# A bilinear stage moved onto column quarters of the matmul array

## The chip, the cores and the metric

The kernel runs on one core of one Trainium2 chip. The time is device microseconds of one launch; the kernel before took 5544.77 us (median of three runs, 5533.71 to 5545.04). The execution that the profile shows spans 5535.1 us. A core has five engines with a queue each: TensorE for matrix products (PE in the profile; its weight loads are shown apart as PEld), VectorE (DVE), ScalarE (ACT), GpSimd (POOL) and SyncE (SP), which here only issues transfers (DMA). They run side by side and wait for each other by semaphores. Data for the engines lie in SBUF, 128 partitions wide; TensorE writes its results to PSUM, which has 128 partitions too.

## The reference

The program is a chain of four layers on an image batch of shape 4 x 96 x 64 x 64. Layer 0 is a state-space block, layers 2 and 3 are a Fourier attention with a feed-forward block. The change concerns layer 1 alone, a bilinear form in every pixel:

```python
s = jax.lax.reduce_window(x, 0.0, jax.lax.add, window_dimensions=(1, 1, K, K), ...)
p = s / float(K * K)
...
p = p.reshape(n, c, ho * wo).transpose(0, 2, 1)
wm = weight * mask
t = jnp.einsum('nlc,ocd->nlod', p, wm)
y = jnp.einsum('nlod,nld->nlo', t, p)
y = y + bias[None, None, :]
```

For each of 4 x 4096 pixels and each of 96 outputs o, y is the sum over all channel pairs (c, d) of wm[o, c, d] p[c] p[d]. The input x is group-normalised first, and y is added to x.

## The kernel before, in words

Since p[c] p[d] is symmetric, the weights of (c, d) and (d, c) are added, and 4656 distinct pairs are left. The kernel holds p as 96 rows (channels) by 4096 columns (pixels) of an image in DRAM, stored twice one below the other, so that rows can be read turned round by any number of channels. Twelve turned copies of 128 rows (`_TURNS`, tiles `turn0` to `turn11`) are loaded for a block of columns. A product of two such copies, element by element, holds p[c] p[d] for 128 channel pairs at once; `_PAIRS` lists the 37 products (copy 0 with itself, then each of copies 6 to 11 with each of copies 0 to 5) that meet every pair. A matmul with 128 rows of weights (`wk`, 37 sets of 128 x 96) sums a product into the 96 outputs; 37 of them accumulate in PSUM.

In `_bilinear` the stage first builds `wk` from weights and masks (L550 to L559). Then it goes over the four images and, in each, over blocks of `CW` = 1024 columns. A block loads its twelve turned copies (L567 and L568, two transfers each, two sets of buffers, so that the next block loads beside the present one). For each k of 37, VectorE multiplies two copies into z (L577; ScalarE squares copy 0 at L575), and two matmuls of 512 columns each (L580) take it up. There are three z buffers. At the block's end VectorE adds the sum and a bias to the image's features (L581). When an image is done, TensorE transposes it in pieces (L587), ScalarE copies them out of PSUM (L588), and a transfer writes them to `tok`.

The order of each engine's queue in this stage is not written out by hand: a scheduler of the framework orders ready instructions by its own model of costs, and puts in the semaphores between tiles. Only the first stage (`_mamba`) writes its order by hand. That stage also holds the one place where two matmuls use different column ranges of the array: `proj` (L214) computes 64 outputs to partitions 0 to 63 and another 64 to partitions 64 to 127 of one PSUM tile.

Of the kernel before, what the change touches and what calls it, by code (L numbers as in the profile page):

```python
# [9 lines left out]
F32 = mybir.dt.float32  # L10
# [3 lines left out]
AF = mybir.ActivationFunctionType  # L14
ALU = mybir.AluOpType
# [4 lines left out]
B, C, L = 4, 96, 4096  # L20
# [9 lines left out]
HID = 384  # L30
NHC = HID // 128
EPS = 1e-5
CW = 1024

# [1 line left out]
_TURNS = [(s, (32 * (i % 3) + 16 * (i // 3)) % C) for i, s in enumerate((0, 76, 60, 44, 32, 88))]  # L38
_TURNS += [(s, 32 * (i % 3) + (2, 6)[i // 3]) for i, s in enumerate((25, 1, 73, 49, 24, 48))]
_PAIRS = [(0, 0)] + [(i, j) for j in range(6, 12) for i in range(6)]  # L40
# [491 lines left out]
def _bilinear(ctx, tc, io, w, f_all, p2, tok):  # L532

    nc = tc.nc
    wp = ctx.enter_context(tc.tile_pool(name="bw", bufs=1))
    stage = ctx.enter_context(tc.tile_pool(name="bst", bufs=1))
    turned = ctx.enter_context(tc.tile_pool(name="bturn", bufs=2))
    work = ctx.enter_context(tc.tile_pool(name="bwork", bufs=3))  # L540
    ps = ctx.enter_context(tc.tile_pool(name="bps", bufs=2, space=PSUM))
    ps_t = ctx.enter_context(tc.tile_pool(name="bpst", bufs=2, space=PSUM))
    bias = w["vec"][:, _V_L1B : _V_L1B + 1]

    NK = 4
    NT = len(_PAIRS)
    wk = wp.tile([128, NT, C], F32, name="wk", tag="wk")
    for k0 in range(0, NT, NK):
        e = min(k0 + NK, NT)
        part = []  # L550
        for n in "12":
            wt = stage.tile([128, NK, C], F32, name=f"wt{n}_{k0}", tag=f"wt{n}")
            mt = stage.tile([128, NK, C], F32, name=f"mt{n}_{k0}", tag=f"mt{n}")
            nc.sync.dma_start(wt[:, : e - k0, :], io["bw" + n][:, k0:e, :])
            nc.sync.dma_start(mt[:, : e - k0, :], io["bm" + n][:, k0:e, :])
            out = wk[:, k0:e, :] if n == "1" else wt[:, : e - k0, :]
            nc.vector.tensor_tensor(out, wt[:, : e - k0, :], mt[:, : e - k0, :], ALU.mult)
            part.append(wt)
        nc.vector.tensor_tensor(wk[:, k0:e, :], wk[:, k0:e, :], part[1][:, : e - k0, :], ALU.add)  # L559

    for b in range(B):
        for q in range(L // CW):
            cols = slice(q * CW, (q + 1) * CW)
            rows = []
            for i, (hi, lo) in enumerate(_TURNS):
                t = turned.tile([128, CW], F32, name=f"turn{i}_{b}_{q}", tag=f"turn{i}")
                nc.sync.dma_start(t[0:C, :], p2[b][hi : hi + C, cols])  # L567
                nc.sync.dma_start(t[C:128, :], p2[b][lo : lo + 128 - C, cols])  # L568
                rows.append(t)
            p_y = ps.tile([C, CW], F32, name=f"py2_{b}_{q}", tag="py2")  # L570
            for k, (i, j) in enumerate(_PAIRS):
                z = work.tile([128, CW], F32, name=f"z_{b}_{q}_{k}", tag="z")
                m = C if i == j else 128
                if i == j:
                    nc.scalar.activation(z[:m], rows[i][:m], AF.Square)  # L575
                else:
                    nc.vector.tensor_tensor(z, rows[i], rows[j], ALU.mult)  # L577
                for n in range(CW // 512):
                    ns = slice(n * 512, (n + 1) * 512)
                    nc.tensor.matmul(p_y[:, ns], wk[:m, k, :], z[:m, ns], start=(k == 0), stop=(k == NT - 1))  # L580
            nc.vector.scalar_tensor_tensor(f_all[b][:, cols], p_y, bias, f_all[b][:, cols], ALU.add, ALU.add)  # L581
        xv = f_all[b].rearrange("c (i j) -> c j i", j=NJ)
        tt = stage.tile([128, NJ, C], F32, name=f"tt{b}", tag="tt", bufs=1)
        for j0 in range(0, NJ, 4):
            p_t = ps_t.tile([128, 4, C], F32, name=f"pt_{b}_{j0}", tag="pst")
            for j in range(4):
                nc.tensor.transpose(p_t[:, j, :], xv[:, j0 + j, :], w["ident"][:C, :C])  # L587
            nc.scalar.copy(tt[:, j0 : j0 + 4, :], p_t)  # L588
        nc.sync.dma_start(tok[b], tt)


def _tokens(ctx, tc, io, w, tok, out):
# [287 lines left out]
@with_exitstack  # L880
def kernel(ctx: ExitStack, tc: tile.TileContext, io, out):
    nc = tc.nc
    cp = ctx.enter_context(tc.tile_pool(name="common", bufs=1))
    dp = ctx.enter_context(tc.tile_pool(name="scratch", bufs=1, space=DRAM))
    w = _shared(nc, cp, io)
    p2 = [dp.tile([2 * C, L], F32, name=f"p2_{b}", tag=f"p2_{b}") for b in range(B)]
    tok = [dp.tile([128, NJ, C], F32, name=f"tok_{b}", tag=f"tok_{b}") for b in range(B)]
    fd = [dp.tile([C, L], F32, name=f"fd_{b}", tag=f"fd_{b}") for b in range(B)]
    with tc.tile_pool(name="stats", bufs=1) as fp:
        fstats = fp.tile([C, B, NCH, 6], F32, name="fstats", tag="fstats")  # L890
        xstats = fp.tile([C, B, NCH, 6], F32, name="xstats", tag="xstats")
        with ExitStack() as c:
            _mamba(c, tc, io, w, fd, fstats, xstats)
        with tc.tile_pool(name="features", bufs=1) as fp2:
            f_all = [fp2.tile([C, L], F32, name=f"f_{b}", tag=f"f_{b}") for b in range(B)]
            with ExitStack() as c:
                _norms_and_pool(c, tc, io, w, f_all, fd, fstats, xstats, p2)
            with ExitStack() as c:
                _bilinear(c, tc, io, w, f_all, p2, tok)
    with ExitStack() as c:  # L900
        _tokens(c, tc, io, w, tok, out)
# [135 lines left out]
```

## Time and profile before

| what | value |
|---|---|
| median time | 5544.77 us |
| span of the profiled execution | 5535.1 us |
| TensorE busy over the span | 4498.7 us (81%) |
| VectorE busy over the span | 4279.5 us (77%) |
| GpSimd busy over the span | 3057.4 us (55%) |
| ScalarE busy over the span | 2553.0 us (46%) |
| first and last start of L580 | 3152.7 and 4221.9 us |
| mean of one multiply L577 (128 x 1024) | 1224 ns |
| mean of one eviction L581 (96 x 1024) | 1280 ns |
| mean of one transpose copy L588 (128 x 384) | 478 ns |

How to read it: an engine's busy share is an average over stages with different limits, so it does not tell what bounds one stage. The profile also gives groups of instructions by line (busy time, mean time of one, and the idle time of the engine just before them with what ended it), the chain of work that ended last, and the busy time of each engine in any stretch of the span. An fp32 matmul stands in the trace as two records of a weight load and a stream each, so that 1184 matmuls of L580 are 2368 records. The end of a matmul in the trace is modelled; the steps from start to start are the safer measure.

### The profile page before, as it was taken

The page shows a single profiled execution, that of the slowest core. Times are in us where ns is not written, and L with a number is a line of the kernel's source. Part 1 is how long each engine was busy: PE and PEld are TensorE (multiplying, and loading weights), DVE is VectorE, ACT ScalarE, POOL GpSimd, SP SyncE. Part 2 cuts the span into 40 slices and gives each one's busy share as a digit, 9 for nine tenths or more (in the row PEclk, how much of TensorE's full clock was granted, in tenths as well). Part 3 has the DMA queues.
Part 4 walks back from the last instruction along what each step waited for, and adds up shares of the span by engine and source line. Part 5 has one row for each costly group of instructions (what it writes and reads, how often), then busy time and mean ns, then how long its engine had stood idle before and what let it go on. Part 6 is the DMA issues. An engine that isn't in the chain of part 4 may idle for free. (4 is left out here: it accounts for less than half of the span.)

```text
span 5535.1 us, 44436 instructions
## 1 busy us (share of the span) xinstructions
PE 4498.7 (81%) x12740; PEld 2034.8 (37%) x12740; DVE 4279.5 (77%) x5316; ACT 2553.0 (46%) x5337; POOL 3057.4 (55%) x2193
## 2 busy tenths in 40 slices
PE   7888888989888988888883099999996777767674
PEld 2333333333333333333321033333332665556462
DVE  5999999999999999999999667767676455556363
ACT  5666767676767666666663000000000434343444
POOL 5999999999999999999994000000000222231313
PEclk9999999999999999999996599999997877768686
DMA  4534444443535353535353463443322000000001
GB/s 97 112 86 102 100 98 104 91 107 87 112 79 123 74 127 68 127 70 124 70 122 107 146 160 99 109 106 95 107 76 80 17 16 16 16 16 16 16 12 46
DMA packets 112892, 461.33 MB, mean 83 GB/s; under 512 B 22660, under 2 KB 30278, under 8 KB 77704
## 3 DMA queue, kind: packets, MB, share of 16 engines
q1 hardware_dynamic: 112648, 458.51, 34.8%
q8 instruction: 100, 1.64, 0.1%
q14 instruction: 144, 1.18, 0.1%
HBM read 422.78 MB, written 35.65 MB: 83 GB/s over the span
## 5 line engine op out<-in xcount | busy, mean ns | idle before, releaser
L373 POOL TENSOR_TENSOR dbx<-du,bq 128x1024 f32<-128x1024 f32 x768 | 1803.2, 2353 | 3.3 <-DMA bq<-rows 3.2
L394 PE MATMUL py<-hc,ident 128*128 128x512 f32 x3072 | 1600.6, 626 | 137.9 <-DVE hc L383 110.6
L367 ACT ACTIVATE da<-delta,aneg 128x512 f32<-128x512 f32 x1536 | 1058.9, 691 | 91.5 <-DVE hs L380 71.5
L380 DVE TENSOR_TENSOR_SCAN da<-da,hst,dbx 128x512 f32<-128x512 f32 x864 | 1099.2, 1272 | 1.2 <-POOL dbx L373 1.2
L580 PE MATMUL py<-z,wk 128*96 128x512 f32 (+1 forms) x2368 | 1022.6, 594 | 82.8 <-DMA mt<-in_bm 43.9
L394 PEld LDWEIGHTS py<-hc,ident 128*128 128x128 f32 x3072 | 554.6, 195 | 1098.3 <-issue 530.9
L383 POOL TENSOR_TENSOR hc<-hs,cq 128x512 f32<-128x512 f32 x672 | 852.9, 1269 | 187.3 <-DVE hs L380 98.6
L577 DVE TENSOR_TENSOR z<-turn,turn 128x1024 f32<-128x1024 f32 x576 | 702.8, 1224 | 302.3 <-PE py L580 276.6
L380 DVE TENSOR_TENSOR_SCAN hs<-da,hst,dbx 128x512 f32<-128x512 f32 x672 | 856.0, 1274 | 9.0 <-ACT da L367 9.0
L707 POOL MEMSET lnT<- 1x512 f32 x64 | 33.2, 520 | 1309.5 <-PE py L580 1237.1
L383 DVE TENSOR_TENSOR hc<-da,cq 128x512 f32<-128x512 f32 x864 | 597.6, 692 | 80.8 <-DMA cq<-rows 4.2
L580 PEld LDWEIGHTS py<-z,wk 128*96 128x96 f32 (+1 forms) x2368 | 386.3, 164 | 709.4 <-issue 624.0
L575 ACT ACTIVATE z<-turn 96x1024 f32<-96x1024 f32 x16 | 16.9, 1056 | 998.9 <-PE py L580 956.5
L387 ACT COPY hst<-da 128x1 f32<-128x1 f32 x864 | 136.2, 158 | 728.1 <-DVE hc L383 718.6
L230 PE MATMUL pc<-xs,taps 128*128 128x512 f32 x768 | 380.7, 592 | 0.0
L840 POOL TENSOR_TENSOR t<-t,o 128x384 f32<-128x384 f32 x64 | 60.3, 942 | 474.9 <-DVE o L838 474.9
L689 POOL TENSOR_SCALAR x_a<-t,m_a,r_a 128x96 f32<-128x96 f32 x256 | 105.6, 427 | 319.8 <-PE plt L705 277.7
L741 PE MATMUL px<-mats,a 128*128 128x128 f32 x768 | 182.4, 403 | 72.6 <-DVE a L730 40.9
L204 PE MATMUL pr<-r,picks 128*96 128x512 f32 x128 | 111.1, 970 | 151.6 <-DVE r L200 151.6
L230 PEld LDWEIGHTS pc<-xs,taps 128*128 128x128 f32 x768 | 145.5, 190 | 185.0 <-issue 174.7
L712 PE MATMUL ph<-w,lnT 97*128 97x192 f32 x512 | 158.5, 478 | 65.6 <-ACT lnT L708 40.3
L214 PE MATMUL pxz<-hn,in_w 96*64 96x512 f32 x768 | 211.6, 622 | 0.0
(231 smaller groups left out, 5179.3 us busy)
## 6 DMA issues: line engine op xcount, KB each, us to landing
bq<-rows SPq DMA_DIRECT2D x256, 512.0 KB, 6.6
cq<-rows SPq DMA_DIRECT2D x256, 512.0 KB, 10.1
turn<-p SPq DMA_DIRECT2D x192, 384.0 KB, 5.6
turn<-p SPq DMA_DIRECT2D x192, 128.0 KB, 5.8
p<-pt SPq DMA_DIRECT2D x8, 1536.0 KB, 10.7
k_fwd<-in_k_fwd SPq DMA_DIRECT2D x32, 256.0 KB, 2.7
k_inv<-in_k_inv SPq DMA_DIRECT2D x32, 256.0 KB, 2.8
x<-in_x SPq DMA_DIRECT2D x16, 384.0 KB, 5.0
```

The costliest lines, as they stand in the source:

```text
L214: nc.tensor.matmul(q[h, :], in_w[:, l, 64 * kk : 64 * kk + 64], hn[b], start=True, stop=True)
L230: nc.tensor.matmul(p_c[k], taps[:, (l * 3 + k) * 4 + j, :], xs[k][:, j : j + TC], start=(j == 0), stop=(j == 3))
L367: nc.scalar.activation(da[u], st[n]["delta"][k], AF.Exp, scale=aneg[:, at : at + 1])
L373: nc.gpsimd.tensor_tensor(t, st[n]["du"][k].unsqueeze(1).to_broadcast([128, 2, TC]), b, ALU.mult)
L380: nc.vector.tensor_tensor_scan(hs[u], da[u], dbx[u], hst[:, at : at + 1], ALU.mult, ALU.add)
L383: (nc.gpsimd if on_pool(u) else nc.vector).tensor_tensor(hc[u], hs[u], c, ALU.mult)
L387: nc.scalar.copy(hst[:, at : at + 1], hs[u][:, TC - 1 : TC])
L394: nc.tensor.matmul(py[n, k], ident, hc.pop(u), start=(s == 0), stop=(s == 15))
L577: nc.vector.tensor_tensor(z, rows[i], rows[j], ALU.mult)
L580: nc.tensor.matmul(p_y[:, ns], wk[:m, k, :], z[:m, ns], start=(k == 0), stop=(k == NT - 1))
L712: nc.tensor.matmul(p_h[:, jj, :], lnT[:, j + jj, :], d["w1"], start=True, stop=True)
L741: nc.tensor.matmul(p_x[:, k, :], a2[:, 128 * m : 128 * m + 128, k0 + k], bd0 if k0 + k == 0 else bd, start=True, stop=True,)
```

## The change

A matmul with 96 outputs uses 96 of the array's 128 columns. The change splits each product into three of 32 outputs, one per column quarter (PSUM partitions 0 to 31, 32 to 63 and 64 to 95), and gives the free fourth quarter (partitions 96 to 127) to the last nine of the 37 products: their three groups of 32 outputs make 27 products of 32, one for each of the first 27 passes. So 28 passes of up to four products are meant to do what 37 did.

The last nine z tiles (the late tiles) are made by GpSimd, one block ahead, and are kept for the whole block. Their sums gather in three PSUM tiles (`acc[0]` to `acc[2]`, all in partitions 96 to 127); ScalarE copies them to `ev`, GpSimd adds `ev` to the features, and VectorE adds the rest as before. Blocks are 512 columns instead of 1024, loads are issued a block ahead, there are four z buffers, and an image's transposes stand after pass 8 of the next image's first block. The three lines of a pass that carry it are L615 (three products of z), L618 (one of a late tile) and L626 (the copy of a finished group).

```diff
-CW = 1024
+CW = 512
...
-    for b in range(B):
-        for q in range(L // CW):
...
-            p_y = ps.tile([C, CW], F32, name=f"py2_{b}_{q}", tag="py2")
-            for k, (i, j) in enumerate(_PAIRS):
-                z = work.tile([128, CW], F32, name=f"z_{b}_{q}_{k}", tag="z")
-                m = C if i == j else 128
-                if i == j:
-                    nc.scalar.activation(z[:m], rows[i][:m], AF.Square)
-                else:
-                    nc.vector.tensor_tensor(z, rows[i], rows[j], ALU.mult)
-                for n in range(CW // 512):
-                    ns = slice(n * 512, (n + 1) * 512)
-                    nc.tensor.matmul(p_y[:, ns], wk[:m, k, :], z[:m, ns], start=(k == 0), stop=(k == NT - 1))
-            nc.vector.scalar_tensor_tensor(f_all[b][:, cols], p_y, bias, f_all[b][:, cols], ALU.add, ALU.add)
+    NP = 28
+    NX = NT - NP
...
+    def make_late(n):
+        k = NP + len(late[n])
+        i, j = _PAIRS[k]
+        z = work.tile([128, CW], F32, name=f"z_{n}_{k}", tag=f"z{k}")
+        nc.gpsimd.tensor_tensor(z, rows[n][i], rows[n][j], ALU.mult)
+        late[n].append(z)
...
+    for n, (b, q) in enumerate(blocks):
+        cols = slice(q * CW, (q + 1) * CW)
+        if n + 1 < len(blocks):
+            load(n + 1)
+        acc = [ps.tile([128, CW], F32, name=f"py{g}_{n}", tag=f"py{g}") for g in range(3)]
+        ev = work.tile([C, CW], F32, name=f"ev_{n}", tag="ev")
+        for p in range(NP):
...
+            z = work.tile([128, CW], F32, name=f"z_{n}_{p}", tag="z", bufs=4)
...
+            for g in range(3):
+                gs = slice(32 * g, 32 * g + 32)
+                nc.tensor.matmul(acc[0][gs, :], wk[:m, p, gs], z[:m], start=(p == 0), stop=(p == NP - 1))
+            if p < 3 * NX:
+                g, k = divmod(p, NX)
+                nc.tensor.matmul(
+                    acc[g][96:128, :],
+                    wk[:, NP + k, 32 * g : 32 * g + 32],
+                    late[n][k],
+                    start=(k == 0),
+                    stop=(k == NX - 1),
+                )
+                if k == NX - 1:
+                    nc.scalar.copy(ev[32 * g : 32 * g + 32, :], acc[g][96:128, :])
+            if n + 1 < len(blocks) and p % 3 == 2:
+                make_late(n + 1)
+            if p == 8 and q == 0 and b > 0:
+                transposes(b - 1)
+        nc.gpsimd.tensor_tensor(f_all[b][:, cols], f_all[b][:, cols], ev, ALU.add)
+        nc.vector.scalar_tensor_tensor(f_all[b][:, cols], acc[0][:C, :], bias, f_all[b][:, cols], ALU.add, ALU.add)
+    transposes(B - 1)
```

## The prediction

> **What bounds the kernel now.** I read the page's costliest groups and its chain first, because the change is confined to one stage (lines 540 to 589) and the question is what that stage waits for.
>
> ```profile
> PE py L580 18%; PE ph L712 2%; PE px L741 2%; PE pa L721 1%; PE pf L833 1%; DVE a L730 1%; ACT y L826 1%; DVE hq L829 1%; PE pv L772 1%; PE plt L705 1%; POOL x_f L689 1%; PE pv L776 1%; DVE r L827 1%; PE pg L791 1%; PE poo L800 1%
> ...
> L580 PE MATMUL py<-z,wk 128*96 128x512 f32 (+1 forms) x2368 | 1022.6, 594 | 82.8 <-DMA mt<-in_bm 43.9
> ...
> L577 DVE TENSOR_TENSOR z<-turn,turn 128x1024 f32<-128x1024 f32 x576 | 702.8, 1224 | 302.3 <-PE py L580 276.6
> ```
>
> One line, the matrix product of L580, is 18% of the chain that ended last. VectorE, which makes its inputs, is busy 702.8 us and idle 302.3 us in the stage, mostly waiting for TensorE to give a z buffer back. Next I cut the stage into stretches; the columns are busy us and count of PE, PEld, DVE, ACT and POOL, then the granted clock.
>
> ```profile
> core 0: us, PE busy (x) PEld busy (x) DVE busy (x) ACT busy (x) POOL busy (x), PEclk, DMA share, GB/s
> ...
> 3400.00:3600.00 200.00, 200.00 (x492) 78.17 (x491) 139.73 (x115) 6.88 (x11) 0.00 (x0) 1.00 0.38 103
> 3600.00:3800.00 200.00, 200.00 (x491) 78.19 (x490) 139.60 (x115) 6.88 (x11) 0.00 (x0) 1.00 0.40 105
> ```
>
> TensorE is busy 200 of 200 us at full clock, GpSimd 0, ScalarE 7, DMA at 0.4. The stage is a bare stream of matmuls from 3195 to 4222 us. An fp32 matmul shows as two records (two loads of weights, two streams). The median step from one record to the next is 0.429 us, so a product of 512 columns costs **0.858 us**, whatever number of outputs it has: 16 blocks x 37 pairs x 2 halves = 1184 products x 0.858 = 1016 us of the stage's 1027.
>
> So the count of 0.858 us slots decides the stage. Does the trace show products side by side in the array? Only for two, in the first stage: L214 writes two sets of 64 outputs, to partitions 0 and 64.
>
> ```profile
> 1521.97 1.08 PE L214 MATMUL pxz<-hn,in_w 96*64 96x512 f32 x4
> 1522.97 2.84 PE L394 MATMUL py<-hc,ident 128*128 128x512 f32 x6
> 1525.75 1.08 PE L214 MATMUL pxz<-hn,in_w 96*64 96x512 f32 x4
> 1526.76 1.13 PE L394 MATMUL py<-hc,ident 128*128 128x512 f32 x2
> 1527.72 0.59 PE L230 MATMUL pc<-xs,taps 128*128 128x512 f32 x1
> ```
>
> Four records (two products) are through in 1.00 us, 1.08 with the tail; a lone product that follows (1526.76) takes 0.96 us to the next. Over all 192 pairs the second product starts a median 7 ns after the first. Two products in different column groups cost one slot.
>
> **What the Trainium skill says.** TensorEngine Tiling (Array Packing), Key Properties: tiles work independently, and changing the mode, not the tile, drains the array. The pairs above agree. TensorE: Matmul & The Clock Gate, Part 3, Measured speedup: three column tiles of 32 outputs ran 2.38 times as fast; no row here has three or four. The same page, What overlaps and what doesn't: matmuls start in program order, strict FIFO. PSUM — Partial Sum Buffer, Engine vs sequencer instructions, says the same of start and completion. The pairs neither prove nor break this for long runs: they only show a neighbour starting 7 ns later.
>
> **The change, part by part.**
>
> (1) Slots intended: 28 passes per 512 columns, each with four products of 32 outputs (three from z_p, one from a late tile), instead of 37 products of 96. At 0.858: 32 blocks x 28 = 896 slots, 769 us.
>
> (2) Slots as queued. This is the step on which the forecast stands. The source puts a late product into each of passes 0 to 26, but the instructions go through a scheduler, and TensorE's queue in the built program is different. In a typical block it holds nine passes of four, then **18 late products in a row** (the last two sets of nine), then 19 passes of three. Around the four image ends the grouping shifts (35 in a row, or blocks with 16), with the same sums. The reason shows in the queue: pass 9's first product waits for a semaphore of ScalarE besides VectorE's. The copy of the finished quarter (acc[0], partitions 96 to 127) at L626 stands before it, as the tile is the same one; the scheduler filled that wait with everything that was ready.
>
> All 18 write partitions 96 to 127. They need the same column group one after another, and with starts in order nothing passes them. Per block: 9 + 18 + 19 = 46 slots; the first triple can start beside the last late product (as the pairs of L214 do): 45. 45 x 32 = 1440 against 1184: 256 more x 0.858 = **+220 us**.
>
> (3) Passes of three or four cost one slot? Lower bound 0.858, the stream. Upper bound: two at a time, as proven here, 1.72. The skill's 2.38 for three speaks for all at once; loads of 32 columns are shorter than the 163 ns of 96. I take 0.858.
>
> (4) VectorE: 27 multiplies of 512 per block. L383 has this shape on VectorE at 692 ns beside a busy GpSimd: 27 x 0.692 = 18.7 us, plus the eviction (1.28 us for 1024 columns, so some 0.75): 19.4 us against 45 x 0.858 = 38.6. Hidden behind TensorE, with four z buffers ahead. In the queue it does two multiplies of the next block before it waits in the eviction, so TensorE has passes 0 to 2 to eat meanwhile: nothing queued behind that wait is late.
>
> (5) GpSimd: nine multiplies and one add per block; L383 on GpSimd, same shape, is 1269 ns: 10 x 1.27 = 12.7 us in 38.6, hidden. Late tiles wait for rows loaded a block ahead. Those issues stand behind the previous block's last multiplies and come at about 0.7 us each in the steady part (pairs every 1.4 to 1.7 us), so the last five pairs land some 10 us into the block, and the late tiles are ready about 13 us in; the earliest late product hoisted from the next block comes 25 slots (21 us) in. No wait.
>
> (6) ScalarE: three copies of 32x512 (L588 copies 384 columns in 478 ns, so about 0.6 each) and a square: 2.5 us, hidden by the 18 late products.
>
> (7) DMA: same bytes, half as long rows; 3.1 MB in 38.6 us is 81 GB/s against 103 now. Hidden.
>
> (8) Ends. The first block waits for half the rows; at the 223 GB/s of the start that would be 14 us, but weights for all pairs are needed by the first pass, so I take 7. In the first nine passes late tiles come at 1.27 us, not 0.86: 9 x 0.41 = +4. Block seams 32 times instead of 16, with a semaphore hop: an estimate of +8 in all (0.15 to 0.3 each). Sum +5.
>
> Sum: 5545 + 220 (2) + 0 (3 to 7) + 5 (8) = 5770; the seams may partly hide behind z buffers that stand ready, so I say **5765 us**, 4% slower.
>
> **The rivals.**
>
> Deep overtaking, faster: the array holds a long reorder window and starts the triples beside the 18 late products. Then all 28 passes count: 32 x 28 = 896 slots, 288 fewer x 0.858 = -247, so **5300**. For it: the intent, independent tiles, and the fact that two records per product still let the neighbour start 7 ns later. Against: both pages state program order, and that neighbour is all that is shown. 14%.
>
> Partial overtaking: the skill (TensorE: Matmul & The Clock Gate, Architectural detail) gives the queue 64 entries with partial reordering. With load and matmul that is 16 products; while 18 late ones drain, about five triples get in: 41 slots, 1312, 128 more: +110, **5655**. If entries count only matmuls, ten get in: 36 slots, -27, about 5520. 15%, of it 3% on the faster side.
>
> Fewer than four side by side: passes of three and four cost two slots. 9x2 + 18 + 19x2 = 74 slots, 2368, twice as many as now: +1016, **6560**; half-way about 6200. Against: the pairs at full overlap. 6%.
>
> The in-order case keeps 65%.
>
> **How the numbers follow.** The in-order case spans 5740 to 5810 (44.5 to 46 slots, seams of 0 to 0.5 us, the start's -10 to +5). Adding the partial case takes the range down to 5510 and the chance held to 80%; overtaking in full and the two-slot case are left out. 5510 to 5830. Faster: 14 + 3 = 17%; same 1%; slower 82%.
>
> **What would show it.** Right: TensorE still busy all through the stage, which lasts about 1250 us; the 18 products of L618 stand 0.86 us apart with no L615 record among them; VectorE and GpSimd mostly wait for TensorE. Step 3 is right if passes of three and four step at 0.86 us. Wrong: L615 records starting between those of a run of L618 (overtaking), or passes at 1.3 us or more (no fourfold overlap), or TensorE idle before L618 with GpSimd named (late tiles late, step 5), or before pass 9 with ScalarE named (step 6). A stage of about 780 us would refute step 2 altogether.

## The result, and the profile after

The changed kernel takes **5916.48 us** (median of four runs, 5908.60 to 5933.61) against 5544.91 us before (four runs, 5533.71 to 5553.07). The ratio is 1.0676, with a 95% interval of 1.0646 to 1.0706. So it is slower, as forecast, but by 372 us where 220 were forecast, and the time lies above the range.

First comes the chain of work that ended last, then the costliest groups. The columns of a group are its count, its busy us and the mean ns of one, and the idle us of its engine just before it with what ended most of that.

```profile
PE py L618 8%; PE py L615 7%; DVE z L612 3%; PE px L785 2%; PE ph L756 2%; DMA turn<-p 2%; PE pa L765 1%; PE pf L877 1%; DVE a L774 1%; ACT y L870 1%; DVE hq L873 1%; PE pv L816 1%; PE plt L749 1%; POOL x_f L733 1%; PE pv L820 1%
...
L612 DVE TENSOR_TENSOR z<-turn,turn 128x512 f32<-128x512 f32 x864 | 843.9, 1011 | 546.7 <-PE py L615 540.3
...
L583 POOL TENSOR_TENSOR z<-turn,turn 128x512 f32<-128x512 f32 x288 | 466.5, 1651 | 886.7 <-DMA turn<-p 885.5
...
L618 PE MATMUL py<-z,wk 128*32 128x512 f32 x1728 | 789.9, 597 | 42.7 <-POOL z L583 42.7
```

The chain holds two things now. The late products (L618) are 8% of it: they run alone, as step (2) said, or they would be hidden under the others. But VectorE's multiply (L612) has come in with 3%, and the groups show why: one lasts 1011 ns in the mean where the forecast took 692, and one of GpSimd's (L583) 1651 ns where it took 1269. The stretches of the stage (us busy and count of PE, PEld, DVE, ACT and POOL, then the granted clock, the DMA share and GB/s) agree:

```profile
3400.00:3600.00 200.00, 182.28 (x1069) 49.01 (x1072) 129.59 (x137) 13.85 (x26) 76.99 (x48) 1.00 0.27 82
3600.00:3800.00 200.00, 182.15 (x1004) 46.37 (x998) 121.68 (x122) 11.12 (x19) 78.55 (x48) 1.00 0.25 73
```

TensorE was busy 200 of 200 us before; now it is 182. The modelled end of a matmul hides more of its idleness, so I took the stage apart by starts. A step of 0.429 us between starts of records is the stream itself; two such steps, 0.858 us, are one slot. What goes beyond a step is waiting.

| first to last start of the stage's products | before | after | difference |
|---|---|---|---|
| the stage, us | 1069 | 1447 | +377 |
| of it, record steps of 0.429 us | 2368 = 1016 us | 2838 = 1217 us | +202 |
| of it, waits (some 40 us of both at the start) | 53 | 230 | +177 |

So there are two losses, near equal: more slots, and waits, of which the forecast had next to none (5 us for the ends of the stage, nothing in its middle). Each has a place in nearly every block. This is the timeline at the beginning of one (start us, us, engine, line, operation, count, and in brackets the idle time ahead with what ended it):

```profile
3604.43 11.93 DVE L612 TENSOR_TENSOR z<-turn,turn 128x512 f32<-128x512 f32 x10
3604.95 8.46 POOL L583 TENSOR_TENSOR z<-turn,turn 128x512 f32<-128x512 f32 x5
3605.60 0.63 PE L615 MATMUL py<-z,wk 128*32 128x512 f32 x3 [0.63 <-DVE z L612]
3605.62 0.62 PE L618 MATMUL py<-z,wk 128*32 128x512 f32 x1
3606.05 0.60 PE L615 MATMUL py<-z,wk 128*32 128x512 f32 x3
3606.07 0.59 PE L618 MATMUL py<-z,wk 128*32 128x512 f32 x1
3607.28 0.63 PE L615 MATMUL py<-z,wk 128*32 128x512 f32 x3 [0.62 <-DVE z L612]
```

A pass of four is what was hoped: four records start at 3605.60 to 3605.62, the second four 0.45 us later. But the next pass begins at 3607.28, 1.68 us after the first. GpSimd is at work (five multiplies in 8.46 us), and VectorE, with ten in 11.93 us, gives TensorE a z too seldom. From start to start the stage has 174 such waits of 0.80 us, six in a typical block; they are 140 of the 190 us of waits that come after its start. The second place is the run of late products; TensorE alone, at the end of one:

```profile
3640.67 2.31 PE L618 MATMUL py<-z,wk 128*32 128x512 f32 x5
3642.39 0.63 PE L615 MATMUL py<-z,wk 128*32 128x512 f32 x3
3642.81 0.59 PE L618 MATMUL py<-z,wk 128*32 128x512 f32 x1
3642.84 0.61 PE L615 MATMUL py<-z,wk 128*32 128x512 f32 x3
3643.24 0.59 PE L618 MATMUL py<-z,wk 128*32 128x512 f32 x1
3643.27 0.61 PE L615 MATMUL py<-z,wk 128*32 128x512 f32 x3
3643.67 0.59 PE L618 MATMUL py<-z,wk 128*32 128x512 f32 x1
3643.70 2.75 PE L615 MATMUL py<-z,wk 128*32 128x512 f32 x18
```

The first triple starts while three records of the run are still to come. So a triple does start ahead of late products that stand before it in the queue, but only at the very end: in all 28 long runs of the trace three records of the run, one and a half products, are still to come.

### The profile page after: what moved, and what is told of

It reads as the page before. It is cut to its first block, busy times and chain, and to the rows that moved or that the text cites. A ratio compares the mean times of both kernels' runs of the same rounds, so it can differ in the third digit from the quotient of the medians.

```text
span 5916.4 us, 55980 instructions
## 1 busy us (share of the span) xinstructions
PE 4752.9 (80%) x17476; PEld 1976.5 (33%) x17476; DVE 4420.3 (75%) x5620; ACT 2611.8 (44%) x5449; POOL 3572.9 (60%) x2513
## 4 chain that ended last, share of the span: by engine, by line
PE 27%; DVE 11%; issue 5%; DMA 4%; ACT 2%; POOL 1%; SPq 1%; ACTq 0%; DVEq 0%; POOLq 0%
PE py L618 8%; PE py L615 7%; DVE z L612 3%; PE px L785 2%; PE ph L756 2%; DMA turn<-p 2%; PE pa L765 1%; PE pf L877 1%; DVE a L774 1%; ACT y L870 1%; DVE hq L873 1%; PE pv L816 1%; PE plt L749 1%; POOL x_f L733 1%; PE pv L820 1%
## 5 line engine op out<-in xcount | busy, mean ns | idle before, releaser
L612 DVE TENSOR_TENSOR z<-turn,turn 128x512 f32<-128x512 f32 x864 | 843.9, 1011 | 546.7 <-PE py L615 540.3
L583 POOL TENSOR_TENSOR z<-turn,turn 128x512 f32<-128x512 f32 x288 | 466.5, 1651 | 886.7 <-DMA turn<-p 885.5
L383 POOL TENSOR_TENSOR hc<-hs,cq 128x512 f32<-128x512 f32 x672 | 852.2, 1268 | 189.0 <-DVE hs L380 102.0
L615 PE MATMUL py<-z,wk 128*32 128x512 f32 (+1 forms) x5376 | 824.9, 600 | 166.8 <-DVE z L612 123.6
L618 PE MATMUL py<-z,wk 128*32 128x512 f32 x1728 | 789.9, 597 | 42.7 <-POOL z L583 42.7
L383 DVE TENSOR_TENSOR hc<-da,cq 128x512 f32<-128x512 f32 x864 | 597.7, 692 | 80.9 <-DMA cq<-rows 4.3
L626 ACT COPY ev<-py 32x512 f32<-32x512 f32 x96 | 55.5, 579 | 929.3 <-PE py L618 770.5
L615 PEld LDWEIGHTS py<-z,wk 128*32 128x32 f32 (+1 forms) x5376 | 199.4, 110 | 725.8 <-DVE z L612 418.4
L618 PEld LDWEIGHTS py<-z,wk 128*32 128x32 f32 x1728 | 166.9, 109 | 417.2 <-issue 365.3
L610 ACT ACTIVATE z<-turn 96x512 f32<-96x512 f32 x32 | 20.2, 631 | 446.6 <-PE py L615 301.1
```

The costliest lines, as they stand in the source:

```text
L383: (nc.gpsimd if on_pool(u) else nc.vector).tensor_tensor(hc[u], hs[u], c, ALU.mult)
L583: nc.gpsimd.tensor_tensor(z, rows[n][i], rows[n][j], ALU.mult)
L612: nc.vector.tensor_tensor(z, rows[n][i], rows[n][j], ALU.mult)
L615: nc.tensor.matmul(acc[0][gs, :], wk[:m, p, gs], z[:m], start=(p == 0), stop=(p == NP - 1))
L618: nc.tensor.matmul(acc[g][96:128, :], wk[:, NP + k, 32 * g : 32 * g + 32], late[n][k], start=(k == 0), stop=(k == NX - 1),)
```

## The experiments

My theory, A in the first expectations: the loss has two causes that can be taken away one by one, the run of late products in TensorE's queue and the multiplies of GpSimd, which slow those of VectorE. Other letters in the expectations are rivals, with what each says beside it. Before took 5541, 5544 and 5553 us in the three sets of runs; each ratio is against before on the same chip.

### One cause away at a time

The late multiplies go to VectorE; the queue stays as the scheduler makes it.

```diff
-        nc.gpsimd.tensor_tensor(z, rows[n][i], rows[n][j], ALU.mult)
+        nc.vector.tensor_tensor(z, rows[n][i], rows[n][j], ALU.mult)
```

> The changed kernel, with the late tiles multiplied by VectorE in place of GpSimd; TensorE's queue keeps its runs of about 18 late products per block. Theory A (two causes: the queue's run of late products costs slots, and VectorE and GpSimd hold each other up when both read two tiles from SBUF): the run stays, about 44 slots per block, 1217 us of slots against 1016 before, but the 190 us of waits for z go; multiplies on VectorE all near 0.69 us; about 5750 us. Theory B (the waits come from block seams, row loads or the ScalarE copy): multiplies on VectorE aren't what ends the waits, so about 5900 us, or more as VectorE has a third more to do. Theory C (contention alone made the change slow, the run costs nothing): below 5560 us.

Measured: 5693.86 us, ratio 1.0262 [1.0237, 1.0287]; 223 us less than the changed kernel. First the stretch from 3200 to 3600 us of the changed kernel, then the same of this one:

```profile
3200.00:3600.00 400.00, 355.23 (x1979) 93.66 (x1974) 248.16 (x245) 24.47 (x44) 147.63 (x96) 0.97 0.25 76
```

```profile
3200.00:3600.00 400.00, 399.07 (x2415) 117.86 (x2410) 254.39 (x400) 29.71 (x52) 18.84 (x11) 1.00 0.30 92
```

VectorE makes 400 instructions instead of 245 in nearly the same busy time: a multiply takes 690 ns in the mean, the late ones too. TensorE is busy 399 of 400 us. The waits of the stage fall from some 190 us to 22, those at its start left out; the slots fall a little too, from 44.3 to 42.4 a block of 512 columns, because the scheduler cuts the runs somewhat differently. So the waits were GpSimd's doing, although TensorE hardly ever waited for GpSimd.

Next the other cause: the queue as the source has it, with the late multiplies on GpSimd.

```diff
+    with tc.manual_schedule():
+        load(0)
...
```

> The changed kernel with the stage's loop under a hand-written order, so that each late product stands in its pass as the source has it; GpSimd still makes the late tiles. Theory A: 28 slots per block (24.0 us) no longer bind; VectorE and GpSimd do: nine pairs at 1.65 us, eighteen multiplies at 0.69, eviction and addition, about 29.5 us per block, 944 us for the stage; about 5470 us. If the two engines did not hinder each other: 25 us per block, 5330 us. If the run in the queue cost nothing: no gain, about 5900 us.

Measured: 5555.01 us, ratio 1.0028 [1.0015, 1.0042]. The slots are 28.0 a block, as intended: 769 us of records instead of 1217. But the waits rise to 268 us, so the expected 5470 is missed. The chains of waits (engine, line, what it waited for: us in total, times, longest) show new ones:

```profile
DVE f L633 <- POOL f L632: 122.4, 32, 3.9
...
PEld py L616 <- ACT ev L627: 47.4, 29, 1.6
...
PEld py L616 <- ACT z L611: 43.7, 31, 1.4
```

In the written order VectorE's last addition (L633) stands in front of the next block's multiplies and waits for GpSimd's addition, 122 us in all; pass 9 waits for ScalarE's copy, and pass 0 for ScalarE's square. The scheduler's runs had filled such waits. VectorE's multiplies still take 994 ns, GpSimd's 1646.

Both together:

```diff
+    with tc.manual_schedule():
...
-        nc.gpsimd.tensor_tensor(z, rows[n][i], rows[n][j], ALU.mult)
+        nc.vector.tensor_tensor(z, rows[n][i], rows[n][j], ALU.mult)
```

> Both at once: order as written, and late tiles multiplied by VectorE. Theory A: VectorE with 36 multiplies of 0.69 us and an eviction of 0.74 us is the bound, 25.7 us per block, with about a microsecond per block for the waits at the seam and for the ScalarE copy; stage about 850 us, about 5380 us. If quarters did not run four at once over a long stretch: 5545 us or more. If VectorE slowed for another reason than GpSimd (other z buffers, shorter rows): about 5470 us as with GpSimd.

Measured: 5670.67 us, ratio 1.0220 [1.0188, 1.0252], 290 us more than expected, although there are 28.0 slots a block and a multiply takes 687 ns. The timeline shows a new wait:

```profile
3718.64 0.69 DVE L583 TENSOR_TENSOR z<-turn,turn 128x512 f32<-128x512 f32 x1 [6.20 <-DMA turn<-p]
...
3719.98 1.08 PE L616 MATMUL py<-z,wk 128*32 128x512 f32 x3 [6.17 <-DVE z L613]
...
3720.84 1.07 PE L616 MATMUL py<-z,wk 128*32 128x512 f32 x3
```

VectorE's queue holds the next block's first late multiply (L583) among this block's, and its rows have not landed: 211 us of wait in 31 blocks, with all that stands behind it. After such a gap of some 6 us the records step by 0.86 us instead of 0.43; the mean granted clock of the run is 0.869. The edit was too blunt to tell the theories apart, and a cleaner one had to undo both.

### Does GpSimd slow VectorE, with nothing else changed?

The kernel before, with work that nobody reads added: a multiply of 448 columns on GpSimd beside every second product.

```diff
                     nc.vector.tensor_tensor(z, rows[i], rows[j], ALU.mult)
+                if k % 2:
+                    junk = work.tile([128, 448], F32, name=f"junk_{b}_{q}_{k}", tag="junk", bufs=1)
+                    nc.gpsimd.tensor_tensor(junk, rows[i][:, :448], rows[j][:, :448], ALU.mult)
```

> The kernel before, with one added multiply of 128x448 on GpSimd beside every second product, of the same two turned tiles into a scratch tile that nobody reads. Theory A (each waits for the other's whole instruction): per two products VectorE needs 2 x 1.22 plus 1.1 to 1.3 us, 3.6 to 3.75 us against TensorE's 3.43; the stage grows by 5 to 9 per cent, 5600 to 5640 us; multiplies on VectorE spread up to 2.5 us. Theory B (no contention): 5545 us, multiplies stay at 1.22 us.

Measured: 5607.19 us, ratio 1.0106 [1.0082, 1.0130]: 62 us from work that nobody waits for. The two groups:

```profile
L577 DVE TENSOR_TENSOR z<-turn,turn 128x1024 f32<-128x1024 f32 x576 | 920.2, 1638 | 153.8 <-PE py L583 134.5
...
L580 POOL TENSOR_TENSOR junk<-turn,turn 128x448 f32<-128x448 f32 x288 | 557.0, 1934 | 651.9 <-DMA turn<-p 632.6
```

VectorE's multiply was 1224 ns with GpSimd idle. Now about half of them take 1225 ns still, and half 2148: 923 more, near GpSimd's shortest multiply here (1128 ns). GpSimd's median is 1992 ns. So each waits for the other; two kinds and no middle suggest a wait for a whole instruction, but two engines in a fixed rhythm could show that with a shared rate too. The changed kernel's own trace decides it, at a place where the two fall out of rhythm:

```profile
3223.16 15.19 DVE L612 TENSOR_TENSOR z<-turn,turn 128x512 f32<-128x512 f32 x5 [15.52 <-PE py L615]
3223.74 1.27 POOL L631 TENSOR_TENSOR f<-f,ev 96x512 f32<-96x512 f32 x1 [17.24 <-ACT ev L626]
3224.97 11.02 POOL L583 TENSOR_TENSOR z<-turn,turn 128x512 f32<-128x512 f32 x9
...
3236.60 1.93 PE L615 MATMUL py<-z,wk 128*32 128x512 f32 x6 [10.94 <-DVE z L612]
```

GpSimd makes an addition and nine multiplies without a gap, 1.22 us from start to start. The second of VectorE's five multiplies starts 0.03 us after that addition and lasts 12.78 us, until 0.55 us after the last of the ten has ended. One engine works at its own pace and the other not at all: a wait, not a shared rate. What decides whether VectorE gets its turn between two instructions of GpSimd, as it mostly does, is not shown.

Does it matter where the inputs lie? These are the multiply that the forecast took as its price, in the kernel before, then VectorE's multiply and its eviction in the changed one (ns: shortest, median, longest):

```profile
L383 DVE TENSOR_TENSOR hc<-da,cq x864: 690/692/693, 69.2 to 2967.1; 128x512 f32<-128x512 f32 x173
...
L612 DVE TENSOR_TENSOR z<-turn,turn x864: 674/692/12776, 3178.2 to 4596.0; 128x512 f32<-128x512 f32 x173
...
L632 DVE SCALAR_TENSOR_TENSOR f<-py,vec,f x32: 734/736/747, 3251.9 to 4599.5; 96x512 f32<-96x512 f32 x32
```

The first and the last have an input in PSUM (`da`, `py`). Of the 864 multiplies of L383, 822 lie over 95% beside work of GpSimd, and none of those takes over 693 ns; 28 of the 32 evictions lie within GpSimd's multiplies of the same stretch, and none of those takes over 741. L612, with both inputs in SBUF, is the one that waits. No run moves one input and leaves all else, so this is a comparison of different instructions. The Trainium skill states the rule: GPSIMD Engine Reference, 1. Specifications, names contention of GpSimd with VectorE instructions that have two inputs in SBUF, and SBUF — State Buffer, Terms, has a port pair that one of the two holds for a whole instruction while the other is blocked. The numbers here agree with both.

### What made the run

Pass 9's first product writes `acc[0]`, and the finished quarter that ScalarE copies just before lies in `acc[0]` too; the framework sees one tile. In this version each late group gathers in the next tile, so that the copy after pass 8 leaves `acc[0]` alone. The order is still the scheduler's; the second kernel has the late multiplies on VectorE too.

```diff
-                    acc[g][96:128, :],
+                    acc[(g + 1) % 3][96:128, :],
...
-                    nc.scalar.copy(ev[32 * g : 32 * g + 32, :], acc[g][96:128, :])
+                    nc.scalar.copy(ev[32 * g : 32 * g + 32, :], acc[(g + 1) % 3][96:128, :])
```

> The changed kernel with one index changed: the first nine late products go to acc[1], the next to acc[2], the last to acc[0], so that pass 9 no longer stands behind ScalarE's copy out of the tile that it adds to. Scheduler's order, late tiles on GpSimd. Theory A (the copy out of acc[0] made the scheduler gather the run): no run of 18 in the queue after the first blocks, 28 slots per block; the two engines' mutual wait remains and bounds at 29 to 32 us per block: 5450 to 5550 us. If the run had another cause: about 5900 us.

> The same index, and the late tiles multiplied by VectorE. Theory A: no run and no contention; VectorE bounds with 36 x 0.69 + 0.74 = 25.6 us, a seam of 1 to 2 us, 27 us per block: about 5400 us, if the scheduler doesn't put a late multiply that waits for row loads ahead of others (that cost 8 us per block in the hand-ordered case). In that case 5600 us or more.

Measured: 5531.35 us, ratio 0.9978 [0.9966, 0.9990], with GpSimd, and 5367.30 us, 0.9683 [0.9658, 0.9709], with VectorE. One index takes the run away: 29.5 and 30.2 slots a block instead of 44.3. With it the four corners are clean, all in the scheduler's order:

| us | late tiles by GpSimd | late tiles by VectorE | the engine costs |
|---|---|---|---|
| run in the queue | 5916 | 5694 | 222 |
| no run | 5531 | 5367 | 164 |
| the run costs | 385 | 327 | |

With the run gone and GpSimd at work, VectorE is the stage's bound for half a block; TensorE alone:

```profile
3500.01 0.63 PE L615 MATMUL py<-z,wk 128*32 128x512 f32 x3 [0.62 <-DVE z L612]
...
3501.70 0.63 PE L615 MATMUL py<-z,wk 128*32 128x512 f32 x3 [0.62 <-DVE z L612]
```

A pass every 1.69 us, the step that the changed kernel shows; here no run of late products hides any of it.

### A version without either cost

The order is written out. Each late tile is multiplied by VectorE just before it is needed and used in three passes running, one for each group of outputs; a block's two additions move into the next block's passes, and the next block's square into pass 14 of the present one; the three copies stand together at the block's end; there are six z buffers. The second kernel differs in one word: the late multiplies are GpSimd's.

```diff
-                g, k = divmod(p, NX)
+                k, g = divmod(p, 3)
+                if g == 0 and k < NX:
+                    extra = multiply(n, NP + k, "late", 3, nc.vector)
...
+                if n and p == 3:
+                    nc.gpsimd.tensor_tensor(features(n - 1), features(n - 1), late[n - 1], ALU.add)
+                if n and p == 6:
+                    nc.vector.scalar_tensor_tensor(
+                        features(n - 1), acc[n - 1][0][:C, :], bias, features(n - 1), ALU.add, ALU.add
+                    )
```

> Hand-written order without the block ahead: each late tile is multiplied by VectorE just before its three products, which take three passes in a row and go to acc[0], acc[1] and acc[2]; the copies out and the additions of a block are put into the next block's passes. Theory A: nothing waits for row loads or seams, VectorE bounds with 25.6 us per block and some 0.6 for the one addition on GpSimd: 26.2 x 32 = 838 us, about 5365 us. If four quarters slow down over long stretches, or ScalarE's copies delay the start of the next block: 5450 us or more.

> The same queues, with only the engine of the nine late multiplies changed to GpSimd. Theory A: in each block nine multiplies of each engine take 1.65 us instead of 0.69 and 1.27, eighteen of VectorE 0.69, eviction 0.74: 29 us per block, 930 us, about 5460 us: an engine more, and slower. If the two engines did not hinder each other: 24.0 us per block by TensorE, about 5310 us, faster than with VectorE alone.

Measured: **5295.40 us**, ratio 0.9553 [0.9522, 0.9584], for the first, the fastest of the study; 5402.43 us, ratio 0.9747 [0.9717, 0.9777], for the second. In the first a stretch of the stage is that of a stage which TensorE bounds:

```profile
3400.00:3600.00 200.00, 199.48 (x1817) 65.41 (x1817) 181.14 (x299) 23.65 (x44) 10.23 (x8) 0.99 0.44 135
```

There are 28.06 slots a block and 19 us of waits. I expected 5365 because 36 multiplies of 0.69 us and an addition, 25.6 us a block, would exceed TensorE's 24.0. But multiplies with nothing to wait for start 602 ns apart though each lasts 680: 36 x 0.602 + 0.74 = 22.4 us, and TensorE stays the bound. With GpSimd as a third engine the kernel is 107 us slower, and the stage from first to last start 97 us (925 for 828): VectorE's multiply takes 1017 ns, and the waits are 116 us.

### How far a triple passes late products

The fast version again, with late products held back and queued in runs of three, or of nine. Theory P says that a product may start ahead of a few of other column groups that stand before it, F that starts are in order.

```diff
+                    held.append((k, g, extra))
+                if len(held) == RUN:
+                    for k, g, extra in held:
+                        gs = slice(32 * g, 32 * g + 32)
+                        nc.tensor.matmul(
+                            acc[n][g][96:128, :], wk[:, NP + k, gs], extra, start=(k == 0), stop=(k == NX - 1)
+                        )
+                    held = []
```

> The hand-written order of the in-time kernel, with late products gathered: three passes of three, then their three late products in a row. Theory P (products of other columns may pass two late products and no more, as the trace of the changed kernel shows at each run's end): the first late one runs beside the last pass, the last two beside the next pass, so a run of three costs nothing: 28 slots, 5295 us. Theory F (strict order of starts): nine groups of four slots, 37 per block, 9 x 0.858 x 32 = 247 us more, 5540 us.

> The same with nine passes, then nine late products in a row. Theory P: 15 slots per group, 46 per block, 18 more, 18 x 0.858 x 32 = 494 us: about 5790 us. Theory F: 16 slots, 49 per block, about 5870 us. If a queue [...]were searched freely: no cost, 5295 us.

Measured: 5322.04 us, ratio 0.9596 [0.9565, 0.9627], for runs of three, and 5740.30 us, 1.0343 [1.0301, 1.0384], for runs of nine. Runs of three cost the stage nothing: 28.05 slots a block, and the stage's last start is at 3981.6 us, against 3981.7 in the version that they were made from. The 27 us between the two medians, which are from different sets of runs, lie after the stage, in code that the edit leaves alone: from the stage's last start to the end of the span it is 1340 us here and 1313 there. The mean granted clock in the first 150 us of that was 0.52 here and 0.72 there. The other three traces with 0.53 to 0.57 there have long ends too, 1330 to 1334 us; the eight with 0.64 or more have 1306 to 1318. So the gap goes with the clock; why the clock differs stays open. Runs of nine cost 43.5 slots. TensorE alone over one group of nine passes and nine late products (L629 the triples, L635 the late ones):

```profile
3703.07 5.33 PE L629 MATMUL py<-z,wk 128*32 128x512 f32 x36
3707.81 0.62 PE L635 MATMUL py<-z,wk 128*32 128x512 f32 x1
3708.22 0.60 PE L629 MATMUL py<-z,wk 128*32 128x512 f32 x3
3708.26 0.59 PE L635 MATMUL py<-z,wk 128*32 128x512 f32 x1
...
3709.12 5.31 PE L635 MATMUL py<-z,wk 128*32 128x512 f32 x12
3713.85 0.63 PE L629 MATMUL py<-z,wk 128*32 128x512 f32 x3
...
3715.16 5.33 PE L629 MATMUL py<-z,wk 128*32 128x512 f32 x36
```

The group takes 3715.16 - 3703.07 = 12.09 us, 14.1 slots where 18 in a row would be 18, 16 with one product side by side at each end, and nine with all; P had forecast 15. Two products overlap at each end. The first late record starts at 3707.81 with three steps of triples still to start, nine records in three column groups; at the other end a triple starts at 3713.85 with three late records still to start. So F falls, and the reach is the same both ways if it is counted in each column group: three records, one and a half products.

## Why the prediction was wrong in size

By its own steps:

(1), (3) **Right.** Passes of four step by one slot, 0.429 and 0.433 us from record to record; the four start within 20 ns of each other in the changed kernel, within 45 in the versions with a written order. The rival with fewer than four side by side is out: five kernels run at 28.0 to 28.1 slots a block.

(2) **Right in mechanism, near in size.** The run stands in the trace, and 44.3 slots a block against the 45 forecast make +202 us for +220. Two things were less exact: the first two triples run beside the last two late products, where the forecast had one beside the last, and so starts are not in strict order. The rival of deep overtaking is out (44.3 slots, not 28), and partial overtaking as the forecast had it, with five or ten triples inside a run, is out too (the reordering in the page that the forecast names for it is of weight loads, not of matmuls). The cause named there, the copy out of `acc[0]`, is shown by the edit of one index that ends the run.

(4) **The step that failed**: "L383 has this shape on VectorE at 692 ns beside a busy GpSimd", and from it "Hidden behind TensorE". The shape was the same and the neighbour was busy, but of L383's two operands, `da` lies in PSUM, and only `cq` in SBUF. Both operands of L612 lie in SBUF. In this trace its median is 692 ns too, but a quarter of its instructions take 1.5 us or more, and the mean is 1011; with GpSimd away the mean is 690. That GpSimd's work is the reason is shown by the extra multiplies in the kernel before and by the three pairs of kernels that differ in that engine (222, 164 and 107 us); that the place of the inputs makes the difference rests on L383 and the eviction L632, which stay at their price beside a busy GpSimd; that a port pair is behind it is the skill's statement. An estimate with the measured step comes near. Each of GpSimd's nine multiplies stretches a pass to 1.68 us for 0.86, 9 x 0.82 = 7.4 us a block, of which z tiles that stand ready can hide at most 3.4 us (four of 0.86): 4.0 to 7.4 us. Measured are 177 us more of waits in 32 blocks, 5.5 a block.

(5) **Right that TensorE would not wait for late tiles**: 9 us past the start. The multiply's price was wrong for the reason in (4), 1651 ns for 1269. The step asked whether GpSimd's work would be ready in time, and not what it does to the engine next to it.

(6), (7) **Right**: 2.4 us of waits for ScalarE's copies, and loads at 73 to 82 GB/s in the two stretches shown.

(8) **Not settled**: the start waits about 40 us in both kernels. Two longer waits soon after it, of some 11 and 7 us, are VectorE shut out for 12.8 and 9.1 us, and so belong to (4). The seams can't be told from the waits of (4) in this trace; all waits of the kernel with VectorE alone, seams in it, are 22 us.

The chance of 82% for slower was well placed; the range was too narrow because step (4) had been given no upper bound. It stood on a row that was taken to be the operation itself, and the bound on the other side, one engine waiting for one instruction of the other in full (0.69 + 1.27 = 1.96 us), was not considered. Of the 864 multiplies two lasted longer even than that.

## What to carry to other kernels

Before work is moved to an idle engine, look at where the operands of both engines lie, not only at their shapes: here a duration measured beside a busy GpSimd with an input in PSUM did not hold for the same shape with both inputs in SBUF. To use free column groups of TensorE, look at its built queue, keep runs of products of one group short (three in a row cost nothing here, nine made the stage 428 us longer), and do not let a copy read a tile that the next product writes, not even in another quarter. Where an idle engine "has room", ask what it holds while it works: here the third engine cost 107 to 222 us and the two alone were enough.

## What the runs showed of the hardware that I had not expected

- Four fp32 products of 32 outputs and 512 columns, in four column groups, take one slot of 0.858 us, like one product; in the changed kernel their records start 6 to 7 ns apart.
- A product may start ahead of products of another column group that stand before it in the queue, by up to three records (one and a half products) of each of those groups, so that two products overlap. The Trainium skill, TensorE: Matmul & The Clock Gate, Part 3, What overlaps and what doesn't, says that matmuls keep strict order in start and end. Here the measurement decides: in 28 of 28 runs a triple starts with three late records still to come, runs of three cost nothing, and groups of nine take 14.1 slots instead of 16. Ends are modelled in these traces, so they say nothing of the order of ends.
- A multiply of VectorE with two fp32 inputs from SBUF and one of GpSimd do not run at once: in turn, 0.69 us becomes up to 1.79 and GpSimd's 1.27 becomes 1.72, in 128 x 512. Out of turn, one multiply of VectorE lasted 12.8 us while GpSimd made ten instructions at its own pace; in the version with the group in another tile one lasted 21.8 us. With one VectorE input in PSUM it is 692 ns beside a busy GpSimd.
- VectorE's multiplies start 602 ns apart with nothing to wait for, and each stands in the trace with 680.
